# A graph network's two layers on one core: where v's sums lie, when h is moved and turned, and when its sums are made

## Chip, core and metric

The kernel runs on one core of a Trainium2 chip. The metric is the device time of one launch in microseconds (us), the median of three runs. TensorE (PE) multiplies matrices into eight PSUM banks; VectorE (DVE) and ScalarE (ACT) read the banks, add, copy and normalise; GpSimd (POOL) adds a bias; DMA queues move data, most of them issued by SyncE (SP).

## What is computed

x has 64 graphs of 256 nodes with 512 features in fp32, adj is 256 x 256. Both layers end in a residual sum.

```python
h = jnp.maximum(_layernorm(x, axis=-1), 0.0)
q = jnp.einsum('bnd,ed->bne', h, Wq); k = jnp.einsum('bnd,ed->bne', h, Wk)
v = jnp.einsum('bnd,ed->bne', h, Wv)
rel = adj.T[None, :, :] * jnp.einsum('bnd,bmd->bnm', q, k)
rel = rel / jnp.linalg.norm(rel, axis=2, keepdims=True)
x = x + jnp.einsum('bnm,bmd->bnd', rel, v)
h = jnp.maximum(_layernorm(x, axis=-1), 0.0)
x = x + jnp.einsum('bnd,do->bno', jnp.einsum('nm,bmd->bnd', adj, h), weight) + bias
```

## The kernel before

**Pairs and stages.** Two graphs make a pair, so there are 32 pairs. The product Wq' Wk is made once (`m_sb`), so that a pair needs g = h M and scores h g'. `first_pairs` fills a software pipeline, `steady` runs 28 times (i = 1 to 28), and `last_pairs` empties it. One call of `steady` works on four pairs at once, and TensorE goes through five stages in it:

1. `attend_and_v(i, ...)`: rel times v of pair i, between the rest of v of pair i+1 and the last product of the layer-1 mix of pair i-1. With stage 5 this is the double stage.
2. `scores(i+1, ...)`: h g' of pair i+1.
3. `g_and_v(i+2, ...)`, called G here: g of pair i+2 and two products of its v.
4. `gather_steps(i, ...)`: adj times the normalised x of pair i, four products `py` copied to `yt` by ACT (L734).
5. `mix_and_v(i, ...)`: y times the layer-1 weight of pair i, between products of v and g of pair i+2.

**Products by sums.** Every large product is one of seven sub-products ("one" to "seven", written `a1`, `c5`, `a6`, `c3`, `a7`, `b2`, `a4` after their banks), in the order of `winograd_steps` (L183). Products 1, 6, 7 and 4 follow each other in `bank_a`, and each partial sum is read out between two of them: product four may start only when the sum after seven has been read. The operands are sums of blocks that DVE makes beforehand: `left_factors` (L172 to L175, factors 7, 5, 6, 3) and `right_operands` (L134 to L137, factors 7, 5, 6, 4). `two_levels` splits two of the seven once more (`g1` to `g4`, in `bank_e` and `bank_d`); its left sums of h are the four steps of `h_second` (tile `hs`, L172 to L175), those of y are `y_second`.

**Order.** PE, DVE and ACT execute in program order. The dictionaries passed to a stage name what DVE and ACT are given after each of its products ("slots" 0 to 6). So an instruction that waits holds up all that was written behind it on its engine.

**What the change touches.**
- `place_blocks` (L433): sixteen DMAs on SP move h of pair i+3 into `blocks`; `transpose_blocks` (L443) makes eight 32x32-block transposes on DVE (L449) into `ht`, and `sums` are h's four left sums. A load of x stands ahead of `place_blocks` on SP's queue.
- `norm_by_scalar` (L347): the first norm on ACT. Its `root` (L368 on DVE, then a square root on ACT, L369) and `end` (L372, L373) give the scale of h; `relus_of_h` writes h (L376).
- `attend_operands` (L631): the factors of rel and v. The three sums of v are written into `blocks` by way of `spare_blocks`.
- `scores`: `placed` holds the moved rel until `turn` (L587) has turned it in stage 5.
- `ln1`: the second norm, with `halves` (L329, L330), `root`, `end`, `relus` (L341 on ACT), `uppers` (L698 on ACT) and `lowers` (L702 on DVE); `add_bias` (L714) runs on POOL and waits for the relu of the same rows, since it writes them in place.

Of the kernel before, what the change touches and what calls it, by code (L numbers as in the profile page):

```python
# [9 lines left out]
F32 = mybir.dt.float32  # L10
# [9 lines left out]
def kernel(  # L20
# [39 lines left out]
    P = 128  # L60
# [3 lines left out]
    NB = 2  # L64
# [18 lines left out]

    ring = [const.tile([P, NB, NC, D], F32, name=f"x_ring{n}") for n in range(5)]
    blocks = const.tile([P, TC, DC, P], F32, name="blocks")

    def load(i, queue=nc.sync):
        X[i] = ring[i % len(ring)]
# [30 lines left out]
    def flat(t):  # L119
        return t.rearrange("p b c d -> p (b c) d")  # L120
# [420 lines left out]
    def scores(i, side={}, by_matmul=False):  # L541


        left, right = HL.pop(i), G.pop(i)
        rel = work.tile([P, NB, NC, N], F32, tag="rel", name=f"rel_{i}")
        placed = work.tile([P, NB, NC, NC, P], F32, tag="placed", name=f"placed_{i}")
        turned = work.tile([P, NB, NC, NC, P], F32, tag="turned", name=f"turned_{i}")
        rn = small.tile([P, NB, NC], F32, tag="rn", name="rn")
        R[i] = turned, rel

        def take(t, k, bank, first):
            dst = rel[:, :, k, ts(t, P)]
            src = bank[:, :HT_].rearrange("p (b m) -> p b m", b=NB)
            if first:
                nc.scalar.copy(dst, src)  # L555
            else:
                nc.vector.tensor_add(dst, src, dst)  # L557

        def mask(k):
            nc.vector.tensor_mul(  # L560
                rel[:, :, k], rel[:, :, k], adjt_sb[:, k : k + 1, :].to_broadcast([P, NB, N])
            )

        def square_sum(b, k):
            nc.scalar.activation(
                placed[:, b, k].rearrange("p t n -> p (t n)"), rel[:, b, k], AF.Square,
                accum_out=rn[:, b, k : k + 1],
            )

        def root():  # L570
            nc.scalar.activation(rn, rn, AF.Sqrt)

        def inverse():
            nc.vector.reciprocal(rn, rn)

        def scale(b, k):
            nc.scalar.activation(rel[:, b, k], rel[:, b, k], AF.Copy, scale=rn[:, b, k : k + 1])

        def place():
            rv = rel.rearrange("p b k (t m) -> p (b k t) m", m=P)  # L580
            pv = placed.rearrange("p b k t n -> p (b k t) n")
            for j in range(P // S):
                for k in range(P // S):
                    nc.sync.dma_start(out=pv[ts(j, S), :, ts(k, S)], in_=rv[ts(k, S), :, ts(j, S)])

        def turn(b, k):
            nc.vector.transpose(turned[:, b, :, k], placed[:, b, k])  # L587

        def each(f):
            return [(lambda b=b, k=k: f(b, k)) for k in range(NC) for b in range(NB)]  # L590

        def turn_at_once():
            for b in range(NB):
                pt = ps_m.tile([P, T], F32, tag="pm", name="pr")
                for t in range(NC):
                    for k in range(NC):
                        nc.tensor.transpose(
                            pt[:, ts(t * NC + k, P)], rel[:, b, k, ts(t, P)], ident
                        )
                nc.scalar.copy(turned[:, b].rearrange("p t k n -> p (t k n)"), pt)  # L600

        winograd(product_of_tokens(left, right), take, side)
        if by_matmul:
            masks = [lambda: mask(0), lambda: mask(1)]
            return masks, each(square_sum), root, inverse, rn, turn_at_once
        return (
            [lambda: mask(0), lambda: mask(1)], each(square_sum), root, inverse, each(scale), place,
            each(turn),
        )
# [21 lines left out]
    def attend_operands(i):  # L631


        turned, rel = R.pop(i)
        v, t = V.pop(i), spare_blocks()
        room = rel.rearrange("p b k m -> p (b k m)")
        left, left_steps = left_factors(
            lambda n, m: turned[:, :, m, n],
            [room[:, ts(j, HT_)].rearrange("p (b n) -> p b n", b=NB) for j in range(3)],
        )  # L640
        right, right_steps = right_operands(
            lambda m, k: v[:, :, m, ts(k, HD)], t
        )
        R[i] = left, right
        return right_steps, left_steps
# [275 lines left out]
    def first_pairs(exact):  # L921
# [49 lines left out]
        if exact:  # L971
# [11 lines left out]
        run(y_steps[0:2])  # L983
        mixed = mix_and_v(0, g, v, {
            0: y_steps[2:4] + totals[0:2], 1: y_second[0:4] + totals[2:4],
            2: w_second_steps[4:8] + y_second[4:8] + v_steps[0:1] + [mean] + row_squares[0:2],
            3: v_steps[1:4] + row_squares[2:4], 4: sums3[2:3] + turns,
            5: sums3[3:4] + rel_steps[0:2],
        })
        return norm0, rel_steps[2:4], mixed, v  # L990

    def steady(i, exact, norm0, rel_steps, mixed, v):

        gs = g_operands(i + 1)
        root0, end0, relu0 = norm0
        relus0 = relus_of_h(i + 3, relu0)
        stats, root, end, relus, uppers, lowers = ln1(i, exact)  # L1000
        halves = [stats[b * NC + t] for t in range(NC) for b in range(NB)]
        attend_and_v(i, mixed, v, {
            0: rel_steps + [root0, end0], 1: relus0[0:2] + gs[0:1], 2: relus0[2:4] + gs[1:2],
            3: gs[2:3], 4: gs[3:4] + halves[0:1], 5: halves[1:2],
        })
        if i + 4 < NP:
# [2 lines left out]
        HL2.pop(i + 1)  # L1009
        h_second = second_h.pop(i + 2)()  # L1010
        masks, squares, norm_root, inverse, scales, place, turns = scores(i + 1, {
            0: halves[2:3], 1: halves[3:4], 2: [root], 3: [end] + relus[0:1], 4: relus[1:2],
            5: uppers[0:1] + h_second[0:2], 6: uppers[1:2] + h_second[2:4],
        })
        turned, sums = transpose_blocks(i + 3)
        bias_steps = add_bias(i)
        g, v = g_and_v(i + 2, {
            0: masks + squares[0:2] + lowers[0:1],
            1: squares[2:4] + [norm_root] + lowers[1:2],
            2: relus[2:4] + [inverse],  # L1020
            3: scales + [place] + turned[0:2],
            4: uppers[2:4] + lowers[2:3] + turned[2:4] + bias_steps[0:2],
            5: lowers[3:4] + turned[4:8] + bias_steps[2:4], 6: sums[0:2],
        })
        v_steps, rel_steps = attend_operands(i + 1)
        y_products, y_steps = gather_steps(i, exact)
        run_steps(y_products, {
            0: sums[2:3], 1: sums[3:4], 2: y_steps[0:1] + v_steps[0:1], 3: v_steps[1:2],
        })
        y_second = second_of_y(i)  # L1030
        totals, row_squares, mean, norm0 = [], [], [], None
        if i + 4 < NP:
            totals, step, row_squares, *norm0 = norm_by_scalar(flat(X[i + 4]))
            mean = [step]
        run(y_steps[1:2])
        mixed = mix_and_v(i, g, v, {
            0: y_steps[2:4] + totals[0:2], 1: y_second[0:4] + totals[2:4],
            2: y_second[4:8] + mean + row_squares[0:2],
            3: turns + row_squares[2:4], 4: rel_steps[0:2], 5: v_steps[2:4],
        })  # L1040
        return norm0, rel_steps[2:4], mixed, v

    def last_pairs(exact, norm0, rel_steps, mixed, v):

        a, b, c = NP - 3, NP - 2, NP - 1
        gs = g_operands(b)
# [5 lines left out]
        })  # L1052
        h_second = second_h.pop(c)()
        masks, squares, norm_root, inverse, scales, place, turns = scores(b, {
            0: halves[2:3], 1: halves[3:4], 2: [root], 3: [end] + relus[0:1], 4: relus[1:2],
            5: uppers[0:1] + h_second[0:2], 6: uppers[1:2] + h_second[2:4],
        })
        g, v = g_and_v(c, {
            0: masks + squares[0:2] + lowers[0:1],
# [10 lines left out]
            0: gs[0:2] + [v["c"]], 1: gs[2:3], 2: gs[3:4], 3: y_steps[0:1], 4: y_steps[1:3],  # L1070
            5: y_steps[3:4] + turns,
        })
        masks, squares, norm_root, inverse, rn, turn_at_once = scores(
            c, {0: [v["g4"]]}, by_matmul=True
        )
        stats, *parts = ln1(b, exact)
        y_second = second_of_y(a, "hs2")
        attend(b, by_slot({n: [stats[n]] for n in range(TC)}, {
            0: y_second[0:4], 1: masks[0:1], 2: masks[1:2] + squares[0:2],
            3: squares[2:4] + y_second[4:8],  # L1080
        }))
        m = mix_by_two_levels(a)
        root, end, relus, uppers, lowers = parts
# [1 line left out]
            m["a1"], m["c5"], lambda: run([m["a6"], m["c"]]), m["g1"], m["a7"], m["g2"], m["a4"],  # L1085
            m["g3"],
        ], {
            0: [norm_root, root], 1: [inverse, end] + relus[0:2], 2: uppers[0:2],
            3: lowers[0:1] + relus[2:3], 4: lowers[1:2] + relus[3:4],
            5: uppers[2:4] + add_bias(b), 6: lowers[2:3], 7: lowers[3:4],  # L1090
        })
        turn_at_once()
        m["g4"]()
        y_steps = gather(b, exact)
        y_second = second_of_y(b, "hs2")
        stats, *parts = ln1(c, exact)
        attend(c, {
            0: [stats[0], y_steps[0]], 1: [stats[1], y_steps[1]], 2: [stats[2]] + y_steps[2:4],
            3: [stats[3]],
        }, rn)  # L1100
        m = mix_by_two_levels(b)
# [2 lines left out]
            m["a1"], m["c5"], lambda: run([m["a6"], m["c"]]), m["g1"], m["a7"], m["g2"], m["a4"],  # L1104
            m["g3"],
        ], {
            0: y_second[0:4] + [root], 1: y_second[4:8] + [end] + relus[0:2] + uppers[0:2],
            2: lowers[0:1] + relus[2:3], 3: lowers[1:2] + relus[3:4],
            4: uppers[2:4] + add_bias(c), 6: lowers[2:3], 7: lowers[3:4],
        })  # L1110
        y_products, y_steps = gather_steps(c, exact)
# [44 lines left out]
```

## Time and profile before

| | |
|---|---|
| time, median of 3 | 1748.74 us (1748.37 to 1749.79) |
| span of the profiled run | 1746.8 us |
| PE busy | 1694.5 us, 97% |
| DVE busy | 1525.6 us, 87% |
| ACT busy | 807.5 us, 46% |
| POOL busy | 191.9 us, 11% |
| granted TensorE clock | 0.998 |
| one period of `steady` (843.52 to 896.68 us) | 53.16 us: PE 51.99, DVE 47.50, ACT 25.72, POOL 5.96 busy |

"Busy" counts the time in which an instruction of the engine is in flight; matmuls overlap, so PE's share says that it is seldom idle, not that it is at its peak. In the timeline a row gives start, duration, engine, line, operation, and in square brackets how long the engine was idle before it and what ended that. The period repeats to 0.01 us over the run, so that one period stands for 28.

### The profile page before, as it was taken

The page shows a single profiled execution, that of the slowest core. Times are in us where ns is not written, and L with a number is a line of the kernel's source. Part 1 is how long each engine was busy: PE and PEld are TensorE (multiplying, and loading weights), DVE is VectorE, ACT ScalarE, POOL GpSimd, SP SyncE. Part 2 cuts the span into 40 slices and gives each one's busy share as a digit, 9 for nine tenths or more (in the row PEclk, how much of TensorE's full clock was granted, in tenths as well). Part 3 has the DMA queues.
Part 4 walks back from the last instruction along what each step waited for, and adds up shares of the span by engine and source line. Part 5 has one row for each costly group of instructions (what it writes and reads, how often), then busy time and mean ns, then how long its engine had stood idle before and what let it go on. Part 6 is the DMA issues. An engine that isn't in the chain of part 4 may idle for free.

```text
span 1746.8 us, 28457 instructions
## 1 busy us (share of the span) xinstructions
PE 1694.5 (97%) x10274; PEld 1532.8 (88%) x10274; DVE 1525.6 (87%) x3336; ACT 807.5 (46%) x1835; POOL 191.9 (11%) x167
## 2 busy tenths in 40 slices
PE   8999999999999999999999999999999999999997
PEld 7978988889888989888898889898888898888976
DVE  6798899888899888998888998889988889988776
ACT  3445444554445554445544445544455544454331
POOL 0011100111101111001111001110011110011111
PEclk9999999999999999999999999999999999999999
DMA  7413332233322333322333322333223333223101
GB/s 239 63 25 85 75 79 66 37 85 81 78 69 53 61 85 77 79 65 48 72 84 75 74 66 44 85 79 79 69 54 61 85 76 77 67 37 61 33 28 51
DMA packets 425734, 122.56 MB, mean 70 GB/s; under 512 B 398064, under 2 KB 398832, under 8 KB 425584
## 3 DMA queue, kind: packets, MB, share of 16 engines
q1 hardware_dynamic: 412992, 80.28, 24.7%
q0 software_dynamic: 8432, 32.51, 4.9%
q10 hardware_dynamic: 4160, 7.87, 1.3%
q8 instruction: 83, 1.36, 0.3%
q14 instruction: 67, 0.55, 0.1%
HBM read 38.27 MB, written 33.55 MB: 41 GB/s over the span
## 4 chain that ended last, share of the span: by engine, by line
PE 75%; DVE 23%; issue 1%; DMA 0%; ACT 0%; ACTq 0%; DVEq 0%
PE bank_a L298 19%; PE bank_a L286 13%; PE bank_c L298 7%; PE bank_a L310 6%; PE bank_a L653 5%; PE bank_e L524 4%; PE bank_c L286 3%; PE bank_d L524 3%; PE bank_c L310 3%; PE bank_e L477 3%; DVE g L486 3%; DVE x_ring L533 2%; PE bank_b L310 2%; PE bank_d L477 2%; PE bank_c L653 1%; PE bank_b L653 1%
## 5 line engine op out<-in xcount | busy, mean ns | idle before, releaser
L714 POOL TENSOR_TENSOR x_ring<-x_ring,bias_bc 128x512 f32<-128x512 f32 x128 | 167.0, 1325 | 750.1 <-ACT h2c L341 750.1
L298 PE MATMUL bank_a<-wv_t,ht 128*128 128x256 f32 x768 | 181.7, 379 | 0.0
L286 PE MATMUL bank_a<-ht,m_t 128*128 128x256 f32 x768 | 181.4, 379 | 0.0
L286 PEld LDWEIGHTS bank_a<-ht,m_t 128*128 128x128 f32 x768 | 145.9, 190 | 19.8
L298 PEld LDWEIGHTS bank_a<-wv_t,ht 128*128 128x128 f32 x768 | 143.5, 190 | 18.3
L363 ACT ACTIVATE blocks<-x_ring,sm 128x512 f32<-128x512 f32 x112 | 80.8, 722 | 147.2 <-DVE sm L360 145.4
L730 PE MATMUL py<-adjt_r,h 128*128 128x256 f32 x1024 | 126.4, 281 | 0.1
L298 PE MATMUL bank_a<-w_t,ys 128*128 128x256 f32 x512 | 121.5, 380 | 3.4 <-DVE x_ring L764 3.4
L730 PEld LDWEIGHTS py<-adjt_r,h 128*128 128x128 f32 x1024 | 120.5, 188 | 0.3 <-DVE h L702 0.3
L341 ACT ACTIVATE h2c<-x_ring,nb,rs 128x512 f32<-128x512 f32 x128 | 97.4, 807 | 43.9 <-DVE nb L338 39.5
L512 ACT COPY v<-bank_a 128x512 f32<-128x512 f32 x96 | 55.5, 578 | 126.8 <-PE bank_a L298 126.8
L298 PEld LDWEIGHTS bank_a<-w_t,ys 128*128 128x128 f32 x512 | 96.8, 190 | 17.6 <-DVE x_ring L764 4.6
L785 POOL DMA_DIRECT2D out_dram<-x_ring x31 | 24.0, 773 | 783.8 <-issue 568.4
L734 ACT COPY yt<-py 128x512 f32<-128x512 f32 x128 | 75.0, 587 | 72.2 <-PE py L730 54.2
L486 DVE TENSOR_TENSOR g<-bank_e,g 128x256 f32<-128x256 f32 x120 | 50.7, 422 | 61.5 <-ACT g L463 31.1
L310 PE MATMUL bank_a<-ht,gt 128*128 128x128 f32 x744 | 98.4, 275 | 0.4 <-DVE rel L557 0.4
L329 DVE BATCH_NORM_STATS2 st<-x_ring 128x6 f32<-128x512 f32 x144 | 97.9, 680 | 0.4
L555 ACT COPY rel<-bank_a 128x256 f32<-128x256 f32 x96 | 35.4, 369 | 132.3 <-PE bank_a L310 132.3
L764 DVE TENSOR_TENSOR x_ring<-bank_a,x_ring 128x512 f32<-128x512 f32 x128 | 86.9, 679 | 6.6 <-PE bank_a L298 6.5
L310 PEld LDWEIGHTS bank_a<-ht,gt 128*128 128x128 f32 x744 | 90.5, 192 | 0.6 <-DVE rel L557 0.6
L449 DVE STREAM_TRANSPOSE ht<-blocks 128x256 f32<-128x256 f32 x248 | 90.5, 414 | 0.6 <-DMA blocks<-h 0.6
L376 ACT ACTIVATE h<-x_ring,nb,rs 128x512 f32<-128x512 f32 x112 | 82.0, 803 | 14.1 <-PE bank_a L653 12.0
(219 smaller groups left out, 4086.2 us busy)
## 6 DMA issues: line engine op xcount, KB each, us to landing
blocks<-h SPq DMA_DIRECT2D x496, 64.0 KB, 2.3
out_dram<-x_ring POOLq DMA_DIRECT2D x31, 1024.0 KB, 4.7
x_ring<-in_x_dram SPq DMA_DIRECT2D x28, 1024.0 KB, 5.2
placed<-rel SPq DMA_DIRECT2D x496, 32.0 KB, 2.0
x_ring<-in_x_dram ACTq DMA_DIRECT2D x4, 1024.0 KB, 5.3
wq_sb<-in_L_gnn_Wq_dram SPq DMA_DIRECT2D x4, 256.0 KB, 4.8
wk_sb<-in_L_gnn_Wk_dram ACTq DMA_DIRECT2D x4, 256.0 KB, 6.1
wv_sb<-in_L_gnn_Wv_dram ACTq DMA_DIRECT2D x1, 1024.0 KB, 5.2
```

Source lines behind the costliest of these rows:

```text
L286: nc.tensor.matmul(bank[:, e * HT_ : (e + 1) * HT_], right[n][:, d, ts(e, P)], left[n][:, d, :], start=(start and e == 0 and d == 0), stop ...
L298: nc.tensor.matmul(bank[:, b * HD : (b + 1) * HD], left[n][:, d, ts(b, P)], right[n][:, d, :], start=(start and b == 0 and d == 0), stop=( ...
L310: nc.tensor.matmul(bank[:, ts(b, P)], right[n][:, d, ts(b, P)], left[n][:, d, ts(b, P)], start=(start and b == 0 and d == 0), stop=(d == H ...
L329: nc.vector.bn_stats(st[:, c, :], src[:, c, :])
L341: nc.scalar.activation(dst, src[:, c, :], AF.Relu, bias=nb[:, c : c + 1], scale=rs[:, c : c + 1])
L449: nc.vector.transpose(ht[:, d, half].rearrange("p (b n) -> p b n", b=NB), by_half[:, :, half, d])
L477: nc.tensor.matmul(out, m_second[k][n], HL2[i][k][n], start=start, stop=True, skip_group_check=True)
L486: nc.vector.tensor_add(dst, sums, dst)
L524: nc.tensor.matmul(out, left[k][n], right[k][n], start=start, stop=True, skip_group_check=True)
L653: nc.tensor.matmul(bank[:, ts(b, HD)], left[n][:, b], right[n][:, b], start=(start and b == 0), stop=True, skip_group_check=True,)
L714: (lambda c=c: add(xt[:, c, :], xt[:, c, :], bias_bc, ALU.add)) for c in range(TC)
L730: nc.tensor.matmul(pm[:, d, :], left[:, b * NC + m, ts(d0 + d, P)], right, start=(n == 0), stop=(n == len(terms) - 1),)
```

## The change

It gives the sums of v a room of their own, so that `blocks` is free for h earlier, and with that it reorders the work of DVE and ACT:

- Two of v's sums lie in `placed` (free once rel is turned), one in a new tile `v_room`. The sums 0 and 1 of v are made in slot 5 of G rather than in the gather stage.
- `root0` and `end0` of the next h are made in slot 4 of stage 5 rather than in slot 0 of stage 1, and its relus one slot earlier.
- h is turned as a whole in slot 1 of G (eight transposes, ahead of `inverse`) rather than in slots 3 to 5; its four sums come in slots 3 and 4 of G rather than in slot 6 and the gather stage.
- In `scores` the steps of `h_second` move from slots 5 and 6 to slots 1 and 2.
- In `last_pairs` the steps of `y_second` and `norm_root`, and the y sums of pair b, move to other slots. `first_pairs` is reordered likewise.

```diff
+    v_room = const.tile([P, D], F32, name="v_room")
...
-        R[i] = turned, rel
+        R[i] = turned, rel, placed
...
-        turned, rel = R.pop(i)
-        v, t = V.pop(i), spare_blocks()
+        turned, rel, placed = R.pop(i)
+        v, spare = V.pop(i), placed.rearrange("p b k t n -> p (b k t n)")
+        t = [
+            r.rearrange("p (b n) -> p b n", b=NB) for r in (spare[:, :D], v_room, spare[:, D:])
+        ]
...
         attend_and_v(i, mixed, v, {
-            0: rel_steps + [root0, end0], 1: relus0[0:2] + gs[0:1], 2: relus0[2:4] + gs[1:2],
+            0: rel_steps + relus0[0:2], 1: relus0[2:4] + gs[0:1], 2: gs[1:2],
             3: gs[2:3], 4: gs[3:4] + halves[0:1], 5: halves[1:2],
...
         masks, squares, norm_root, inverse, scales, place, turns = scores(i + 1, {
-            0: halves[2:3], 1: halves[3:4], 2: [root], 3: [end] + relus[0:1], 4: relus[1:2],
-            5: uppers[0:1] + h_second[0:2], 6: uppers[1:2] + h_second[2:4],
+            0: halves[2:3], 1: halves[3:4] + h_second[0:1], 2: [root] + h_second[1:4],
+            3: [end] + relus[0:1], 4: relus[1:2], 5: uppers[0:1], 6: uppers[1:2],
         })
...
+        v_steps, rel_steps = attend_operands(i + 1)
         g, v = g_and_v(i + 2, {
             0: masks + squares[0:2] + lowers[0:1],
-            1: squares[2:4] + [norm_root] + lowers[1:2],
-            2: relus[2:4] + [inverse],
-            3: scales + [place] + turned[0:2],
-            4: uppers[2:4] + lowers[2:3] + turned[2:4] + bias_steps[0:2],
-            5: lowers[3:4] + turned[4:8] + bias_steps[2:4], 6: sums[0:2],
-        })
-        v_steps, rel_steps = attend_operands(i + 1)
+            1: squares[2:4] + [norm_root] + lowers[1:2] + turned + [inverse],
+            2: relus[2:4],
+            3: scales + [place] + sums[0:2],
+            4: uppers[2:4] + lowers[2:3] + sums[2:4] + bias_steps,
+            5: lowers[3:4] + v_steps[0:2],
+        })
         y_products, y_steps = gather_steps(i, exact)
-        run_steps(y_products, {
-            0: sums[2:3], 1: sums[3:4], 2: y_steps[0:1] + v_steps[0:1], 3: v_steps[1:2],
-        })
+        run_steps(y_products, {2: y_steps[0:1]})
...
-            totals, step, row_squares, *norm0 = norm_by_scalar(flat(X[i + 4]))
-            mean = [step]
+            totals, step, row_squares, root0, end0, relu0 = norm_by_scalar(flat(X[i + 4]))
+            mean, ends = [step], [root0, end0]
...
-            3: turns + row_squares[2:4], 4: rel_steps[0:2], 5: v_steps[2:4],
+            3: turns + row_squares[2:4], 4: rel_steps[0:2] + ends, 5: v_steps[2:4],
...
         masks, squares, norm_root, inverse, rn, turn_at_once = scores(
-            c, {0: [v["g4"]]}, by_matmul=True
+            c, {0: [v["g4"]], 1: y_second[0:4], 2: y_second[4:8]}, by_matmul=True
         )
...
         attend(b, by_slot({n: [stats[n]] for n in range(TC)}, {
-            0: y_second[0:4], 1: masks[0:1], 2: masks[1:2] + squares[0:2],
-            3: squares[2:4] + y_second[4:8],
+            0: masks[0:1], 1: masks[1:2] + squares[0:2], 2: squares[2:4], 3: [norm_root],
         }))
...
-            0: y_second[0:4] + [root], 1: y_second[4:8] + [end] + relus[0:2] + uppers[0:2],
-            2: lowers[0:1] + relus[2:3], 3: lowers[1:2] + relus[3:4],
+            0: y_second[0:4] + [root], 1: [end] + relus[0:2] + uppers[0:2],
+            2: y_second[4:8] + lowers[0:1] + relus[2:3], 3: lowers[1:2] + relus[3:4],
```

More of the change, by code (lines that the diff above doesn't have):

```diff
@@ L985, in first_pairs, with steady @@
             0: y_steps[2:4] + totals[0:2], 1: y_second[0:4] + totals[2:4],
-            2: w_second_steps[4:8] + y_second[4:8] + v_steps[0:1] + [mean] + row_squares[0:2],
-            3: v_steps[1:4] + row_squares[2:4], 4: sums3[2:3] + turns,
-            5: sums3[3:4] + rel_steps[0:2],
-        })
-        return norm0, rel_steps[2:4], mixed, v
-    def steady(i, exact, norm0, rel_steps, mixed, v):
+            2: w_second_steps[4:8] + y_second[4:8] + [mean] + row_squares[0:2],
+            3: v_steps[0:2] + row_squares[2:4], 4: turns + rel_steps[0:2] + norm0[0:2],
+            5: v_steps[2:4] + sums3[2:4],
+        })
+        return norm0[2], rel_steps[2:4], mixed, v
+    def steady(i, exact, relu0, rel_steps, mixed, v):
         gs = g_operands(i + 1)
-        root0, end0, relu0 = norm0
         relus0 = relus_of_h(i + 3, relu0)
@@ L1016, in steady @@
         bias_steps = add_bias(i)
+        v_steps, rel_steps = attend_operands(i + 1)
         g, v = g_and_v(i + 2, {
             0: masks + squares[0:2] + lowers[0:1],
-            1: squares[2:4] + [norm_root] + lowers[1:2],
-            2: relus[2:4] + [inverse],
-            3: scales + [place] + turned[0:2],
-            4: uppers[2:4] + lowers[2:3] + turned[2:4] + bias_steps[0:2],
-            5: lowers[3:4] + turned[4:8] + bias_steps[2:4], 6: sums[0:2],
+            1: squares[2:4] + [norm_root] + lowers[1:2] + turned + [inverse],
[3 more added lines that the diff above has]
+            5: lowers[3:4] + v_steps[0:2],
         })
-        v_steps, rel_steps = attend_operands(i + 1)
         y_products, y_steps = gather_steps(i, exact)
-        run_steps(y_products, {
-            0: sums[2:3], 1: sums[3:4], 2: y_steps[0:1] + v_steps[0:1], 3: v_steps[1:2],
-        })
+        run_steps(y_products, {2: y_steps[0:1]})
         y_second = second_of_y(i)
-        totals, row_squares, mean, norm0 = [], [], [], None
+        totals, row_squares, mean, ends, relu0 = [], [], [], [], None
         if i + 4 < NP:
-            totals, step, row_squares, *norm0 = norm_by_scalar(flat(X[i + 4]))
-            mean = [step]
+            totals, step, row_squares, root0, end0, relu0 = norm_by_scalar(flat(X[i + 4]))
+            mean, ends = [step], [root0, end0]
         run(y_steps[1:2])
@@ L1038, in steady, with last_pairs @@
             2: y_second[4:8] + mean + row_squares[0:2],
-            3: turns + row_squares[2:4], 4: rel_steps[0:2], 5: v_steps[2:4],
+            3: turns + row_squares[2:4], 4: rel_steps[0:2] + ends, 5: v_steps[2:4],
         })
-        return norm0, rel_steps[2:4], mixed, v
-    def last_pairs(exact, norm0, rel_steps, mixed, v):
+        return relu0, rel_steps[2:4], mixed, v
+    def last_pairs(exact, relu0, rel_steps, mixed, v):
         a, b, c = NP - 3, NP - 2, NP - 1
@@ L1054, in last_pairs @@
         masks, squares, norm_root, inverse, scales, place, turns = scores(b, {
-            0: halves[2:3], 1: halves[3:4], 2: [root], 3: [end] + relus[0:1], 4: relus[1:2],
-            5: uppers[0:1] + h_second[0:2], 6: uppers[1:2] + h_second[2:4],
+            0: halves[2:3], 1: halves[3:4] + h_second[0:1], 2: [root] + h_second[1:4],
+            3: [end] + relus[0:1], 4: relus[1:2], 5: uppers[0:1], 6: uppers[1:2],
         })
@@ L1072, in last_pairs @@
         })
+        y_second = second_of_y(a, "hs2")
         masks, squares, norm_root, inverse, rn, turn_at_once = scores(
-            c, {0: [v["g4"]]}, by_matmul=True
+            c, {0: [v["g4"]], 1: y_second[0:4], 2: y_second[4:8]}, by_matmul=True
         )
         stats, *parts = ln1(b, exact)
-        y_second = second_of_y(a, "hs2")
         attend(b, by_slot({n: [stats[n]] for n in range(TC)}, {
-            0: y_second[0:4], 1: masks[0:1], 2: masks[1:2] + squares[0:2],
-            3: squares[2:4] + y_second[4:8],
+            0: masks[0:1], 1: masks[1:2] + squares[0:2], 2: squares[2:4], 3: [norm_root],
         }))
@@ L1087, in last_pairs @@
         ], {
-            0: [norm_root, root], 1: [inverse, end] + relus[0:2], 2: uppers[0:2],
+            0: [root], 1: [inverse, end] + relus[0:2], 2: uppers[0:2],
             3: lowers[0:1] + relus[2:3], 4: lowers[1:2] + relus[3:4],
@@ L1093, in last_pairs @@
         m["g4"]()
-        y_steps = gather(b, exact)
+        y_products, y_steps = gather_steps(b, exact)
+        run_steps(y_products, {2: y_steps[0:1]})
         y_second = second_of_y(b, "hs2")
@@ L1097, in last_pairs @@
         attend(c, {
-            0: [stats[0], y_steps[0]], 1: [stats[1], y_steps[1]], 2: [stats[2]] + y_steps[2:4],
+            0: [stats[0], y_steps[1]], 1: [stats[1], y_steps[2]], 2: [stats[2], y_steps[3]],
             3: [stats[3]],
```

## The prediction

> **What bounds the kernel now.** I read the busy shares first: PE 97%, DVE 87%. Then the chain of waits, which names what is left between PE's instructions.
>
> ```profile
> PE 1694.5 (97%) x10274; PEld 1532.8 (88%) x10274; DVE 1525.6 (87%) x3336; ACT 807.5 (46%) x1835; POOL 191.9 (11%) x167
> ...
> PE 75%; DVE 23%; issue 1%; DMA 0%; ACT 0%; ACTq 0%; DVEq 0%
> ```
>
> PE carries three quarters of the chain and DVE nearly all of the rest: at some places of each period PE waits for DVE. PE's timeline of one period (53.16 us, from 843.52) finds them.
>
> ```profile
> 861.77 1.89 PE L298 MATMUL bank_a<-w_sb,yt 128*128 128x256 f32 x8
> 864.47 1.97 PE L298 MATMUL bank_c<-w_sb,yt 128*128 128x256 f32 x8 [0.81 <-DVE yt L173]
> ...
> 878.92 0.61 PE L524 MATMUL bank_d<-wvt_sb,hs 128*128 128x128 f32 x4
> 879.88 1.13 PE L653 MATMUL bank_a<-blocks,rel 128*128 128x256 f32 x4 [0.34 <-DVE rel L174]
> ...
> 888.23 0.61 PE L524 MATMUL bank_d<-wvt_sb,ht 128*128 128x128 f32 x4
> 888.85 1.13 PE L653 MATMUL bank_a<-blocks,turned 128*128 128x256 f32 x4
> ```
>
> Unhindered, eight 256-column matmuls start 1.73 us apart, four of 128 columns 0.445. So mix product c5 could start at 863.50 and is 0.97 late, attend's six at 879.37 and is 0.51 late, attend's four at 888.67 and is 0.18 late; each refills more slowly too, by 0.07 to 0.10. Together 1.93 us per period, and that is all PE loses: over 28 periods 54 us is the most that any reordering of DVE can win here.
>
> DVE's timeline shows why c5 waits, and what its own slow places are.
>
> ```profile
> 843.00 1.14 DVE L172 TENSOR_TENSOR hs<-ht 128x256 f32<-128x256 f32 x1
> 844.07 1.48 DVE L173 TENSOR_TENSOR hs<-ht 128x256 f32<-128x256 f32 x1
> ...
> 861.10 0.69 DVE L175 TENSOR_TENSOR ht<-ht 128x512 f32<-128x512 f32 x1
> 861.71 0.68 DVE L172 TENSOR_TENSOR ys<-yt 128x512 f32<-128x512 f32 x1
> 862.31 0.68 DVE L134 TENSOR_TENSOR blocks<-v 128x512 f32<-128x512 f32 x1
> 863.03 0.69 DVE L135 TENSOR_TENSOR v<-v 128x512 f32<-128x512 f32 x1
> 863.64 0.68 DVE L173 TENSOR_TENSOR yt<-yt 128x512 f32<-128x512 f32 x1
> ...
> 880.20 0.16 DVE L368 TENSOR_SCALAR sq<-sq 128x4 f32<-128x4 f32 x1
> 880.63 0.18 DVE L372 RECIPROCAL rs<-rs 128x4 f32<-128x4 f32 x1 [0.27 <-ACT rs L369]
> 880.85 0.16 DVE L373 TENSOR_TENSOR nb<-sm,rs 128x4 f32<-128x4 f32 x1
> ```
>
> The yt sum that c5 needs stands behind h's four sums and two of v. And `h_second`'s first two steps take 1.14 and 1.48 us, where the same forms take 0.42 in the first call (98.43, 98.76). POOL's timeline gives the reason:
>
> ```profile
> 842.60 2.67 POOL L714 TENSOR_TENSOR x_ring<-x_ring,bias_bc 128x512 f32<-128x512 f32 x2 [14.95 <-ACT h2c L341]
> ```
>
> Both lie inside POOL's two bias adds. Each ends 0.21 to 0.28 us after one of them.
>
> **What the Trainium skill says.** "SBUF — State Buffer", Who interferes with whom: a DVE instruction with two SBUF inputs contends with a GpSimd instruction that reads SBUF, and the later one blocks. The trace agrees: 0.42 becomes 1.14 and 1.48 beside POOL, while transposes (one input) and reads of PSUM keep their times at 850.79 to 853.3, beside the second pair of bias adds. "PSUM — Partial Sum Buffer", Engine vs sequencer instructions: DVE and ACT are strict first-in first-out; DVE's order in the trace is that of the slots. Same page, PSUM bank collisions: a bank has to be guarded as a whole, so product four waits for the read after seven; the trace has it at 888.85, just after L660 ends at 888.80, and at 87.16 in `scores`, where four waited 0.41 for L557.
>
> **The change, part by part** (us on the clock of the period above; a DVE step followed by an independent one costs 0.60 for 512 columns, 0.33 for 256, a dependent one 0.72 and 0.45).
>
> 1. *Gather and mix.* Four h sums (2.8) and two v sums (1.3) leave the gather stage. The last copy of `yt` ends at 862.55, L173 then starts at 862.58; before, 0.83 lay between L173's start and c5's, so c5 is fed by 863.41, ahead of 863.50. Gain 0.97 + 0.07 = 1.04.
>
> 2. *`root0` and `end0` in mix slot 4.* From L368 to the next instruction they take 0.72 (880.20 to 880.92), of which 0.27 is DVE waiting for ACT's root. Between 873.88, where DVE waits for PE (`g4`), and 879.82, where L174 feeds six, DVE never idles. So the trio pushes everything behind it (four reads of x, two v sums, L174), and six starts 0.72 later against PE's other work: cost 0.72. Behind L174 the trio is gone, so DVE is where it was (L660 at 880.93 against 880.92). Seven, now 0.72 later, ends at 888.67, L660 reads it by 889.40 and four could start at 889.40: the wait at four is gone, and four moves from 888.85 to 889.43. Net cost in attend 0.58. The alternative to this, that it is hidden, needs idle DVE in that stretch, and there is none.
>
> 3. *`h_second` in slots 1 and 2 of `scores`.* POOL's adds start only after relu L341 (895.75), so at 893 the port is free, and I take 0.42 each: L172 892.97, L333 893.30, L173 893.38, L174 893.83, L175 894.29. Queued behind them are L557 for c3 (894.63, before 894.11), `end` (894.97 to 895.25) and L557 for a7, ending at 895.67. Product four wants 895.62: it waits about 0.1, plus 0.1 of refill. Cost 0.2. If all were as slow as before (1.07 + 1.52 to the next start instead of 0.33 + 0.45), L557 would end at 897.5 and the wait would be 2.0.
>
> 4. *G.* With a1 of G at 0: relus come 0.5 later, POOL's first adds fall on -0.4 to 2.2, so the first mask (two SBUF inputs) ends near 2.7, the second at 3.3, two lowers by 4.5, eight transposes (0.333 each) by 7.15, `inverse`, two g1 adds by 7.95 (before 7.35), two h sums by 10.4 (one blocked by POOL's second adds), c and a7 by 11.5, while a4 needs a7's read at 12.15. Then g2, lower, two sums, lower (14.4; the second gather product needs it at 15.6), two v sums (15.75), g3's adds by 16.8 (before 15.6). PE waits nowhere, unless a gather product takes the bank that the last add frees: 0 to 0.4. I take 0.1. L173 of the gather stage can start at 19.2, so 2 us of DVE room remain, enough for L172 (0.68).
>
> 5. *h's move.* Its relus end about 881, but the sixteen DMAs stand behind the load of x on SP (884.86). Issue takes 11.4 (890.05 to 901.42), landing 2.3: they are done by 898.9, and the transposes want them near 901. The x load (5.2) shares the engines; still hidden. New rooms for v's sums cost nothing: `placed` is free after `turns`, `v_room` is last read by seven. ACT (25.72 of 53.16 busy) hides the earlier relus.
>
> Sum per period: -1.04 + 0.58 + 0.2 + 0.1 = -0.16, over 28 periods -4.5. The last `steady` call has no next norm, so 0.7 more is won there.
>
> 6. *`last_pairs`.* `y_second` (2 x 1.03) in `scores(c)` delays L557 of a7 to 1673.86, against four at 1673.42: cost 0.5. Without it in `attend(b)` the read of mix a1 comes near 1684.9 instead of 1686.3, so a6 no longer waits 1.58 (+0.17): start 1685.1 against 1686.38, net gain 1.25 after that cost. In pair c's attend one y sum less ahead of a1's read (0.6 of the 1.05 wait), and a6's read ahead of `y_second[4:8]` (1.05) removes most of the 0.78 wait before a7; the two overlap with later waits for ACT: gain about 1. Together -2.2. `first_pairs`: L173 and L174 of rel change places with h and v sums in one queue: 0.
>
> Total -4.5 - 0.7 - 2.2 = -7.4: 1748.7 - 7.4 = 1741.
>
> **Rivals.**
> - *More is won.* The trio hides after all and nothing waits in `scores`: -1.04 and the 0.28 of four per period, 28 x -1.3 = -36 and -3 at the end, at best 1710; with half of it, about 1724. For it: DVE totals 47.50 of 53.16, so there is room on average. Against: no idle DVE from 873.88 to 879.82.
> - *DVE backlog in G (slower).* G's queue gets 4.1 us more and had only 2.65 idle; if the locks or a late h add 1 to 2 us, c5's wait returns or the gather products wait for a bank: +0.88 per period, 25 - 3 gives about 1771; a mild form, about 1757. For it: part 4 ends 1.2 later than before. Against: 2 us remain ahead of L173.
> - *`h_second` stays slow (slower).* If not POOL but reading `ht` beside PE makes it slow: +1.8 per period, 50 - 7, about 1791. Against: 0.42 at 98.43 with PE reading `ht` as well, and 0.41 at 1640.30 just as POOL starts.
> - *Cancels.* The delays of parts 2 to 4 add up to 1.04: 1746.
>
> **How the numbers follow.** Forecast with its small variations (1734 to 1745) 45%, more won 20%, cancels 13%, backlog 17%, `h_second` slow 5%. The predicted time is 1741. The range 1720 to 1762 takes in half of the larger gain and a mild backlog. Faster by over 0.2% (below 1745.2): forecast nearly whole and more won, 0.62; within: 0.16; slower (above 1752.2): 0.22.
>
> **What would show it.** Right: c5 of mix without a wait for L173, six waiting about 1.2 for L174, four of attend with none, a four in `scores` that waits 0.1 to 0.3 for L557, `hs` steps of 0.42, a period near 53.0. Wrong: any wait of PE in G or gather, `hs` steps over 1 us in `scores`, the transposes L449 waiting for the DMA of h, or six no later than before.

## The result, and the profile after

| | before | after |
|---|---|---|
| time, median of 4 runs each on the same chip | 1748.55 us (1748.24 to 1749.79) | 1742.72 us (1741.9 to 1743.3) |
| span of the profiled run | 1746.8 us | 1740.6 us |
| mean period of `steady` (second to 29th gather) | 53.16 us | 52.92 us |

The ratio is 0.9965 with a 95% interval of 0.9948 to 0.9982: faster by a third of a per cent. Lines of the kernel after are one higher than before's from L86 on and five higher from L636 on; the edits of the experiments shift the later lines by a few, at most nine.

These are the busy shares and the chain of waits of the kernel after:

```profile
PE 1698.9 (98%) x10274; PEld 1531.7 (88%) x10274; DVE 1523.9 (88%) x3336; ACT 818.3 (47%) x1835; POOL 198.2 (11%) x167
...
PE 84%; DVE 14%; issue 1%; ACT 0%; DMA 0%; ACTq 0%; DVEq 0%
```

PE's part of the chain has risen from 75% to 84% and DVE's has fallen from 23% to 14%, so some waits for DVE are gone, and not all. PE's timeline of one period says which. G begins in it at 840.65 and again at 893.67 us: it is one of six longer periods (53.02 instead of 52.89), in which the gather products take 3.86 us instead of 3.73.

```profile
859.20 1.89 PE L299 MATMUL bank_a<-w_sb,yt 128*128 128x256 f32 x8
860.92 1.90 PE L299 MATMUL bank_c<-w_sb,yt 128*128 128x256 f32 x8
...
873.79 0.49 PE L525 MATMUL bank_e<-w_t,yt 128*128 128x128 f32 x2
...
875.64 0.61 PE L525 MATMUL bank_d<-wvt_sb,hs 128*128 128x128 f32 x4
...
876.98 1.13 PE L658 MATMUL bank_a<-placed,rel 128*128 128x256 f32 x4 [0.72 <-DVE rel L175]
...
885.33 0.61 PE L525 MATMUL bank_d<-wvt_sb,ht 128*128 128x128 f32 x4
885.83 1.13 PE L658 MATMUL bank_a<-placed,turned 128*128 128x256 f32 x4
...
891.71 1.06 PE L311 MATMUL bank_b<-ht,g 128*128 128x128 f32 x8
892.68 1.16 PE L311 MATMUL bank_a<-ht,gt 128*128 128x128 f32 x8
```

Mix product c5 follows its predecessor after 1.72 us and waits no longer. Attend's six, 0.445 after its predecessor if unhindered, is now 0.89 late (876.98 - 876.09; before 0.51), and `g4` ahead of it loses another 0.24 and refills 0.1 longer. Four of attend is 0.05 late instead of 0.18, and four of `scores` (892.68) is 0.08 late and takes 1.16 instead of 1.06.

DVE's timeline shows the two things that the change was to mend, and a new one:

```profile
841.63 2.23 DVE L561 TENSOR_TENSOR rel<-rel,adjt_sb 128x512 f32<-128x512 f32 x2 [1.42 <-ACT rel L556]
...
849.27 1.65 DVE L174 TENSOR_TENSOR ht<-ht 128x512 f32<-128x512 f32 x1
...
858.13 0.69 DVE L173 TENSOR_TENSOR ys<-yt 128x512 f32<-128x512 f32 x1 [0.89 <-ACT yt L739]
860.01 0.69 DVE L174 TENSOR_TENSOR yt<-yt 128x512 f32<-128x512 f32 x1 [1.19 <-ACT yt L739]
...
872.42 0.18 DVE L373 RECIPROCAL rs<-rs 128x4 f32<-128x4 f32 x1 [0.27 <-ACT rs L370]
...
876.50 0.42 DVE L175 TENSOR_TENSOR rel<-turned 128x256 f32<-128x256 f32 x1
...
889.95 0.39 DVE L173 TENSOR_TENSOR hs<-ht 128x256 f32<-128x256 f32 x1
890.33 0.42 DVE L174 TENSOR_TENSOR hs<-ht 128x256 f32<-128x256 f32 x1
```

The yt sum now finds DVE idle (0.89 and 1.19 us), and `h_second`'s first steps take 0.4 instead of 1.14 and 1.48. In their place the masks of rel (a mean of 1106 ns instead of 683) and two sums of h (means of 879 and 1528 ns instead of 680 and 692) lie beside POOL's bias adds. The root and end, with their 0.27 of idling (872.42), now lie ahead of L175, which feeds six.

The ledger by the first gather product of each pair: it starts 0.63 us earlier for the first pair; the next interval is 1.36 longer (58.58 against 57.22); the 27 periods after that win 6.58; the last three intervals change by -0.91, -0.77 and +1.44, and the tail by -0.1. The sum is -6.2. The first 0.63 is no gain of the change: the kernel of the fifth experiment, which is before's up to that point, starts its first gather at 109.08 us, just as the kernel after does, where before started it at 109.71; over all eleven traces this start scatters from 109.03 to 110.79.

### The profile page after: what moved, and what is told of

The parts are those of the page before. It is cut to its first block, busy times and chain, and to the rows that moved or that the text cites. A ratio compares the mean times of both kernels' runs of the same rounds, so it can differ in the third digit from the quotient of the medians.

```text
span 1740.6 us, 28453 instructions
## 1 busy us (share of the span) xinstructions
PE 1698.9 (98%) x10274; PEld 1531.7 (88%) x10274; DVE 1523.9 (88%) x3336; ACT 818.3 (47%) x1835; POOL 198.2 (11%) x167
## 3 DMA queue, kind: packets, MB, share of 16 engines
q8 instruction: 83, 1.36, 0.3%
## 4 chain that ended last, share of the span: by engine, by line
PE 84%; DVE 14%; issue 1%; ACT 0%; DMA 0%; ACTq 0%; DVEq 0%
PE bank_a L299 22%; PE bank_a L287 13%; PE bank_a L311 7%; PE py L735 6%; PE bank_c L299 6%; PE bank_a L658 5%; PE bank_e L525 4%; PE bank_c L287 3%; PE bank_e L478 3%; PE bank_d L525 3%; PE bank_c L311 3%; PE bank_d L478 2%; DVE x_ring L534 2%; PE bank_b L311 2%; DVE x_ring L769 1%; PE bank_b L658 1%
## 5 line engine op out<-in xcount | busy, mean ns | idle before, releaser
L719 POOL TENSOR_TENSOR x_ring<-x_ring,bias_bc 128x512 f32<-128x512 f32 x128 | 173.2, 1374 | 736.5 <-DVE rel L558 443.8
L769 DVE TENSOR_TENSOR x_ring<-bank_a,x_ring 128x512 f32<-128x512 f32 x128 | 86.9, 679 | 21.7 <-PE bank_a L299 21.5
L561 DVE TENSOR_TENSOR rel<-rel,adjt_sb 128x512 f32<-128x512 f32 x64 | 68.4, 1106 | 41.3 <-ACT rel L556 41.3
L665 DVE TENSOR_TENSOR x_ring<-bank_a,x_ring 128x512 f32<-128x512 f32 x116 | 78.8, 679 | 10.7 <-PE bank_a L658 10.7
```

The lines of the kernel that those rows point to most:

```text
L719: (lambda c=c: add(xt[:, c, :], xt[:, c, :], bias_bc, ALU.add)) for c in range(TC)
L769: nc.vector.tensor_add(xt[block], bank.rearrange("p (b e) -> p b e", b=NB), xt[block])
```

## Experiments

The runs of before beside them had medians of 1748.70, 1748.64 and 1748.56 us, one for each group of runs.

### The trio alone goes back

```diff
-            3: turns + row_squares[2:4], 4: rel_steps[0:2] + ends, 5: v_steps[2:4],
+            3: turns + row_squares[2:4], 4: rel_steps[0:2], 5: v_steps[2:4],
...
-            0: rel_steps + relus0[0:2], 1: relus0[2:4] + gs[0:1], 2: gs[1:2],
+            0: rel_steps + ends0 + relus0[0:2], 1: relus0[2:4] + gs[0:1], 2: gs[1:2],
```

The trio (the three DVE instructions of `root0` and `end0`: L369, L373, L374) goes back in `first_pairs` in the same way; the lines that hand the steps over are left out here.

> The changed kernel with root0 and end0 back in slot 0 of attend, behind the four sums of rel. Theory (DVE never idles between g4 and L175, so the trio delays six): L175 comes 0.72 earlier, six starts about 0.7 earlier (876.25 in place of 876.98 on the period's clock), four about 0.5 earlier; period 52.4 in place of 52.9, time 1728 to 1731. Rival (the trio has to come early so that h is moved in time): its relus start about 1 us later, the transposes L450 in G wait for the DMA of h, and the time is 1742 or more.

Measured: 1726.57 us (1725.47 to 1728.08), ratio 0.9876 (0.9859 to 0.9892), mean period 52.32, 0.6 below the kernel after. Six waits a visible 0.34 instead of 0.72:

```profile
867.76 1.13 PE L658 MATMUL bank_a<-placed,rel 128*128 128x256 f32 x4 [0.34 <-DVE rel L175]
```

And `g4` follows its predecessor after 0.87 us, without a delay. So `root0` and `end0` in slot 4 cost 0.6 per period, and without that edit the change is worth 1.2%. The first interval, which has the same trio in `first_pairs`, falls from 58.58 to 57.96.

### `h_second` goes back to slots 5 and 6

```diff
-            0: halves[2:3], 1: halves[3:4] + h_second[0:1], 2: [root] + h_second[1:4],
-            3: [end] + relus[0:1], 4: relus[1:2], 5: uppers[0:1], 6: uppers[1:2],
+            0: halves[2:3], 1: halves[3:4], 2: [root], 3: [end] + relus[0:1], 4: relus[1:2],
+            5: uppers[0:1] + h_second[0:2], 6: uppers[1:2] + h_second[2:4],
```

The same lines change in `last_pairs`.

> The changed kernel with h_second back in slots 5 and 6 of scores. Theory: four of scores no longer waits (0.2 per period won); two hs steps lie beside POOL's bias adds again and take over 1 us, the masks come free of them, G's queue ends about 1 us later, which the 2.1 us of DVE idle ahead of the yt sum L174 take up: period 0.2 shorter, about 1737 to 1739. Rival (G is full, h_second had to leave it): c5 of mix or a product of G waits, 1745 to 1760.

Measured: 1751.26 us (1748.52 to 1754.94), ratio 1.0013 (1.0004 to 1.0022), mean period 53.18. The theory was wrong and the rival right. DVE's and then PE's timeline of this run, in G:

```profile
846.24 1.14 DVE L173 TENSOR_TENSOR hs<-ht 128x256 f32<-128x256 f32 x1
847.30 1.49 DVE L174 TENSOR_TENSOR hs<-ht 128x256 f32<-128x256 f32 x1
...
855.37 1.71 DVE L173 TENSOR_TENSOR ht<-ht 128x512 f32<-128x512 f32 x1
...
858.33 0.68 DVE L466 TENSOR_TENSOR g<-bank_a,g 128x512 f32<-128x512 f32 x1
```

```profile
857.01 1.89 PE L299 MATMUL bank_c<-wvt_sb,ht 128*128 128x256 f32 x8
859.06 1.99 PE L287 MATMUL bank_a<-ht,m_t 128*128 128x256 f32 x8 [0.16 <-DVE g L466]
```

The steps of `hs` are slow again, the queue behind them is late, and product four of G, due at 857.01 + 1.73 = 858.74, starts at 859.06, when the read of `bank_a` after seven (858.33 to 859.01) is over. That is 0.32 late, with 0.1 of refill; 0.18 is won back at four of `scores`; the net 0.24 is the difference of the periods (53.13 against 52.89 in the usual period). The first interval is longer too, 60.56 against 58.58; what makes it so was not traced. I had judged G's room by the 2 us that DVE idles at its end. The room that counts lies in its middle: in the kernel after, the same read ends at 852.12 and four starts at 852.80, 0.68 later.

### The sums of v in `blocks` again

```diff
-        v, spare = V.pop(i), placed.rearrange("p b k t n -> p (b k t n)")
-        t = [
-            r.rearrange("p (b n) -> p b n", b=NB) for r in (spare[:, :D], v_room, spare[:, D:])
-        ]
+        v, t = V.pop(i), spare_blocks()
```

> The changed kernel with v's sums in blocks again. Theory (the room is what lets h be moved early): the DMAs of h start only after four of attend (886.8), land at about 900.5 where the transposes want 898.0; DVE waits about 2.5 us in slot 1 of G, and PE about 1.9 per period behind it: 1790, at least 1765. Rival (h's move was hidden anyway): within 5 us of the changed kernel.

Measured: 1757.73 us (1757.26 to 1760.15), ratio 1.0055 (1.0038 to 1.0072). The periods scatter from 52.88 to 54.41 with a mean of 53.47, which is 0.55 above the kernel after: the direction is right, the size is a third of what I expected. This is SyncE's queue and then a part of DVE's timeline of this run:

```profile
890.89 0.38 SPq L90 DMA_DIRECT2D x_ring<-in_x_dram  x1
895.78 11.33 SPq L440 DMA_DIRECT2D blocks<-h  x16
```

```profile
855.45 2.73 DVE L450 STREAM_TRANSPOSE ht<-blocks 128x256 f32<-128x256 f32 x8 [1.79 <-DMA blocks<-h]
```

The move of h (here that of the next period) now starts 4.9 us after the load of x, when product four of attend, which reads `blocks`, is over (894.58 to 895.71), and DVE idles 1.79 us for it ahead of the transposes. Little of that reaches PE in this period: the two sums of h behind the transposes now miss the bias adds (0.67 and 0.69 instead of 0.91 and 1.65), and the read after seven ends 0.67 us later in G than in the kernel after, which had 0.68 to spare. Product four of G is 0.05 late (861.46) and refills 0.1 longer. In the longest period, 54.41 us, DVE waits longer, and PE too:

```profile
480.70 2.73 DVE L450 STREAM_TRANSPOSE ht<-blocks 128x256 f32<-128x256 f32 x8 [3.16 <-DMA blocks<-h]
...
483.41 0.39 DVE L487 TENSOR_TENSOR g<-bank_e,g 128x256 f32<-128x256 f32 x1
```

```profile
480.92 1.89 PE L287 MATMUL bank_a<-ht,m_t 128*128 128x256 f32 x8
483.85 0.71 PE L478 MATMUL bank_e<-hs,m_t 128*128 128x128 f32 x4 [1.04 <-DVE g L487]
```

The product in `bank_e`, due at 482.65, is 1.20 late with 0.1 of refill, and four is 0.13 late with 0.1: 1.53 together, and 54.41 - 52.89 = 1.52. So the room for the sums of v is what lets h be turned early: without it the early turning stalls DVE, and PE pays for what exceeds the room in G.

### Before, without the bias adds

```diff
-        return [
-            (lambda c=c: add(xt[:, c, :], xt[:, c, :], bias_bc, ALU.add)) for c in range(TC)
-        ]
+        return [lambda: None for c in range(TC)]
```

> The kernel before without the bias adds on POOL (the bias is left out of the result). Theory (port lock): the hs steps L172 and L173 take 0.42 in place of 1.14 and 1.48, and since DVE waits for PE at the end of G in any case, the period stays at 53.16 and the time within 2 us of 1748. Rival (they are slow because PE reads ht at that time): they stay over 1 us.

DVE's timeline of this run, `h_second` in its old place:

```profile
844.17 0.42 DVE L172 TENSOR_TENSOR hs<-ht 128x256 f32<-128x256 f32 x1
844.51 0.42 DVE L173 TENSOR_TENSOR hs<-ht 128x256 f32<-128x256 f32 x1
```

Without POOL's adds the steps take 0.42 where they took 1.14 and 1.48. That the adds slow them is thereby shown; that the two engines contend for SBUF when a DVE instruction has two inputs there is what "SBUF — State Buffer", Who interferes with whom, of the Trainium skill states. The time did not fall with it: 1753.19 us (1752.95 to 1756.92), ratio 1.0029 (1.0018 to 1.0041), period 53.30 against 53.16. So in before those slow steps cost PE nothing. The 0.14 more goes with L368, which takes 0.31 us (a mean of 315 ns over its 28 calls) instead of 0.16 and stands ahead of the read that four of attend waits for (0.33 late instead of 0.18):

```profile
881.37 0.31 DVE L368 TENSOR_SCALAR sq<-sq 128x4 f32<-128x4 f32 x1
```

Why L368 takes longer stays open.

### Before, with `h_second` early and nothing else

```diff
-            0: halves[2:3], 1: halves[3:4], 2: [root], 3: [end] + relus[0:1], 4: relus[1:2],
-            5: uppers[0:1] + h_second[0:2], 6: uppers[1:2] + h_second[2:4],
+            0: halves[2:3], 1: halves[3:4] + h_second[0:1], 2: [root] + h_second[1:4],
+            3: [end] + relus[0:1], 4: relus[1:2], 5: uppers[0:1], 6: uppers[1:2],
```

The same lines change in `last_pairs`.

> The kernel before with h_second alone moved to slots 1 and 2 of scores. Theory: hs steps 0.42 each, four of scores waits about 0.1 for L557 and refills 0.1 slower, the room won in G is idle DVE: period 53.36, time about 1754. Rival (DVE's total is the bound): the 1.8 us of lock time taken out show as a shorter period, under 1740.

Measured: 1754.28 us (1753.5 to 1756.46), ratio 1.0033 (1.0019 to 1.0047), mean period 53.34: 0.18 more than before, as expected: four of `scores` is 0.08 late with 0.1 of refill. The same edit costs 0.18 per period in the kernel before and saves 0.24 in the kernel after (the second experiment). Before, the slow steps put 1.8 us more in front of a G that had room for them. After, six more of the transposes and two sums of h stand ahead of the read that product four of G waits for, and it has not.

### The ends in another order

In `first_pairs` the sums of h and v go ahead of the rel sums in the last slots of the mix; in `last_pairs` the second half of `y_second` of pair b goes back by one slot.

```diff
-            2: w_second_steps[4:8] + y_second[4:8] + [mean] + row_squares[0:2],
-            3: v_steps[0:2] + row_squares[2:4], 4: turns + rel_steps[0:2] + norm0[0:2],
-            5: v_steps[2:4] + sums3[2:4],
+            2: w_second_steps[4:8] + y_second[4:8] + v_steps[0:1] + [mean] + row_squares[0:2],
+            3: v_steps[1:2] + row_squares[2:4], 4: sums3[2:3] + turns + v_steps[2:4],
+            5: sums3[3:4] + rel_steps[0:2] + norm0[0:2],
...
-            0: y_second[0:4] + [root], 1: [end] + relus[0:2] + uppers[0:2],
-            2: y_second[4:8] + lowers[0:1] + relus[2:3], 3: lowers[1:2] + relus[3:4],
+            0: y_second[0:4] + [root], 1: y_second[4:8] + [end] + relus[0:2] + uppers[0:2],
+            2: lowers[0:1] + relus[2:3], 3: lowers[1:2] + relus[3:4],
```

> The changed kernel with first_pairs' mix slots in the old order (new rooms kept) and y_second[4:8] of pair b back in slot 1 of mix b. Theory: 1.3 us at the start (six and g4 of the first double stage) and 1.4 us at the end (the wait of 2.41 ahead of g2) come back: about 1740. Rival (the new order pays elsewhere in these stages): 1742 to 1744.

Measured: 1742.1 us (1740.3 to 1743.82), ratio 0.9961 (0.9947 to 0.9975). The last interval falls from 27.56 to 25.37, and the first rises from 58.58 to 59.78: one half right, one wrong. What had gone wrong at the end is seen in the kernel after, on DVE, POOL and PE:

```profile
1706.73 1.02 DVE L175 TENSOR_TENSOR ys<-yt 128x128 f32<-128x128 f32 x1
1707.79 1.24 DVE L176 TENSOR_TENSOR ys<-yt,ys 128x128 f32<-128x128 f32 x1
```

```profile
1706.34 2.54 POOL L719 TENSOR_TENSOR x_ring<-x_ring,bias_bc 128x512 f32<-128x512 f32 x2 [15.17 <-ACT h2c L342]
```

```profile
1710.55 0.71 PE L525 MATMUL bank_e<-w_t,ys 128*128 128x128 f32 x4 [2.41 <-DVE x_ring L534]
```

Two steps of `y_second`, which take 0.28 us elsewhere, take 1.02 and 1.24 inside POOL's bias adds, and PE then waits 2.41 us for the read of x queued behind them. With the steps back by one slot they take 0.28 and 0.29, ahead of POOL's adds, and PE waits 0.61, as in before:

```profile
1706.72 0.29 DVE L176 TENSOR_TENSOR ys<-yt,ys 128x128 f32<-128x128 f32 x1
```

```profile
1711.08 0.71 PE L525 MATMUL bank_e<-w_t,ys 128*128 128x128 f32 x4 [0.61 <-DVE x_ring L534]
```

The change took `h_second` out from beside the bias adds and put `y_second` there.

### The sums of v ahead of attend

The third sum of v is made at the end of the gather stage, in a room behind `ys2`, and the fourth after the rel sums in attend; neither lies ahead of L175 any more. The lines that hand the room over are left out here.

```diff
-        run(y_steps[1:2])
+        run(y_steps[1:2] + v_steps[2:3])
...
-            3: turns + row_squares[2:4], 4: rel_steps[0:2] + ends, 5: v_steps[2:4],
+            3: turns + row_squares[2:4], 4: rel_steps[0:2] + ends,
...
-        return relu0, rel_steps[2:4], mixed, v
+        return relu0, rel_steps[2:4] + v_steps[3:4], mixed, v
```

> The changed kernel with v's sum 2 (factor 6) made at the end of the gather stage, into room behind ys2 in the h2 tile, and sum 3 (factor 4) behind the sums of rel in attend. Theory (six waits for DVE's queue alone, and DVE has idle time before mix): L175 comes 1.3 earlier, six starts without a wait, four about 1.0 earlier: period 51.9, time about 1715. Rival (DVE is full from mix to attend, so that work moved from ahead of six only shifts the wait to seven, four or a6): period above 52.5, time above 1732.

Measured: 1718.37 us (1716.18 to 1719.07), ratio 0.9826 (0.9809 to 0.9842), usual period 51.92 as expected. Six now follows its predecessor after 0.44 us. The trio stays in slot 4, and its cost has become smaller, not nothing; PE's timeline of a period has it at `g4`:

```profile
860.44 1.03 PE L662 MATMUL bank_a<-v,turned 128*128 128x256 f32 x4
861.55 0.49 PE L525 MATMUL bank_e<-w_t,yt 128*128 128x128 f32 x2
```

In the run with the trio back 0.87 lay between these two starts, here 1.11, and `g4` refills 0.1 longer: 0.34 per period, as in the kernel after. The read of `bank_e` that stands behind the trio ends at 861.49.

### All together, and then with `first_pairs` left alone

The sums of v as above; `root0` in slot 4 and `end0` behind the rel sums; the ends as in the run of the ends.

> The kernel of the run before with, besides, root0 alone in slot 4 of mix and end0 behind the sums of rel in attend (so that DVE does not wait for ACT's root), and both ends as in the run that restores them. Theory: the 0.34 that g4 of mix loses is won too, 9 us, and 2.7 at the ends: about 1703. Rival (full DVE): above 1725.

Measured: 1708.56 us (1705.02 to 1711.78), ratio 0.9762 (0.9745 to 0.9778), usual period 51.58 or 51.70. Against the run before, 51.92 - 51.58 = 0.34 is won: `end0`, with its wait for ACT's root, no longer stands ahead of the read that `g4` needs. The first interval is 61.1 us. The last run therefore leaves the slots of `first_pairs` as the change has them, but for its root and end:

```diff
-            3: v_steps[0:2] + row_squares[2:4], 4: turns + rel_steps[0:2] + norm0[0:2],
+            3: v_steps[0:2] + row_squares[2:4], 4: turns + rel_steps[0:2],
...
-        return norm0[2], rel_steps[2:4], mixed, v
+        return (norm0[2], norm0[0:2]), rel_steps[2:4], mixed, v
...
-            0: rel_steps + relus0[0:2], 1: relus0[2:4] + gs[0:1], 2: gs[1:2],
+            0: rel_steps[0:2] + ends0 + rel_steps[2:] + relus0[0:2], 1: relus0[2:4] + gs[0:1], 2: gs[1:2],
```

> Same as the run with everything together, but first_pairs keeps the slots of the changed kernel, and its root and end follow the first pair of rel sums of attend in slot 0. Theory: the first interval, from the first gather to the second, which took 61.1 us there, comes near the 57.96 us of the run with the trio alone moved back; the steady periods stay at 51.58 to 51.70 and the last interval at 25.4; time 1708.6 - 3 = 1705 to 1706. Rival: the first interval is long because v's third and fourth sums, now also made late, and the first pair's sums of h fill one queue whatever the order; then it stays above 60 and the time at 1708 to 1709.

Measured: 1706.6 us (1705.08 to 1706.8), ratio 0.9756 (0.9743 to 0.9769). The first interval is 59.53, between the two theories: what remains over 57.96 is not settled. The time alone does not tell the last two runs apart, as their ranges overlap. The busy shares, the chain of waits, and one period by engine (length; busy PE, PEld, DVE, ACT, POOL; clock; DMA) of this last kernel:

```profile
PE 1685.9 (99%) x10274; PEld 1532.4 (90%) x10274; DVE 1513.4 (89%) x3336; ACT 818.2 (48%) x1835; POOL 198.1 (12%) x167
...
PE 94%; DVE 4%; issue 0%; DMA 0%; ACT 0%; ACTq 0%; DVEq 0%
```

```profile
843.50:895.08 51.58, 51.58 (x322) 47.39 (x321) 47.09 (x105) 26.05 (x59) 6.22 (x5) 1.00 0.34 73
```

PE is busy for all of the 51.58 us. The prediction's unhindered period is 53.16 - 1.93 = 51.23, so 0.35 of the 1.93 remains. The view shows no idle time in it, but the starts do, at four of attend and four of `scores`:

```profile
869.04 0.61 PE L525 MATMUL bank_d<-wvt_sb,ht 128*128 128x128 f32 x4
869.54 1.13 PE L662 MATMUL bank_a<-placed,turned 128*128 128x256 f32 x4
...
875.42 1.06 PE L311 MATMUL bank_b<-ht,g 128*128 128x128 f32 x8
876.38 1.16 PE L311 MATMUL bank_a<-ht,gt 128*128 128x128 f32 x8
```

They are 0.05 and 0.07 late, and each refills 0.1 longer: 0.32 together.

## Why the prediction came out as it did

The total was right (1741 forecast, 1742.7 measured), and in the period so were the mechanisms. In the two ends the forecast missed, and an error of the other sign in the period's sum (step 4, 0.1 in each period) and the 0.6 at the start made up for most of it. That the total came within 2 us is in this part luck.

1. *Gather and mix* (1.04): c5 waits no longer, and the yt sum finds DVE idle. Right.
2. *The trio* (net 0.58): six and `g4` together are now 0.89 + 0.34 = 1.23 late against 0.51, a step of the 0.72 forecast. Taking the trio back won 0.6. Right in the sum, and shown by the run; the forecast put all 0.72 at six, and the trace has 0.34 of it at `g4`. That VectorE's queue is strictly first in, first out is what "PSUM — Partial Sum Buffer", Engine vs sequencer instructions, of the Trainium skill says, so that an instruction that waits for ACT holds up all behind it; the 0.27 at 872.42 is such a wait.
3. *`h_second`* (0.2): 0.42 a step, four of `scores` 0.08 late with 0.1 of refill. Right in time and, by the run without bias adds, in cause.
4. *G* (0.1): PE waits nowhere in it, so 0. With that the sum is -0.26, and 52.89 is measured in the usual period against 53.16. The step had both numbers, 0.65 us before a4 and 2 us at the end; that the smaller one is the room was shown only by the run with `h_second` late, where it was used up.
5. *h's move* (0): hidden, though in another order than forecast: the relus of h end at 877.24, not near 881. SP's queue shows four of the sixteen DMAs issued ahead of the load of x:

```profile
877.27 4.92 SPq L440 DMA_DIRECT2D blocks<-h  x4
882.65 0.37 SPq L90 DMA_DIRECT2D x_ring<-in_x_dram  x1
883.06 10.63 SPq L440 DMA_DIRECT2D blocks<-h  x12
```

6. *The ends* (-2.2, and 0 in `first_pairs`) is the step that failed. The last `steady` call won its 0.7 (53.08 to 52.17, with the period's gain). Then pair b and pair c together came out at -0.77 + 1.44 - 0.1 = +0.57 instead of -2.2: I had counted the `y_second` steps by their number and not asked what POOL does beside them, though step 3 rests on just that. Put back by one slot, they give back 2.2. `first_pairs` came out at +1.36 instead of 0 (the 0.63 before it is not the change's). Of the 1.36, 0.62 is its own trio in slot 4 (the first run). The other order of its sums that I tried was worse by 1.2, so what the rest is stays open.

In the forecast's sum: 27 periods gave 6.6 instead of 4.3, the last `steady` call 0.9 as forecast (its period's gain and 0.7), and the two ends cost 1.36 + 0.57 = 1.9 instead of winning 2.2. With the 0.6 at the start that is 6.2 in the span instead of 7.4.

Of the rivals, "more is won" did not come, because the trio does not hide, as its counter-argument said; the last run, with the sums of v and the root and end elsewhere, shows that a gain of that size was there to be had, 1706.6 against the 1710 of that rival at best. "DVE backlog in G" did not come either, but the run with `h_second` late is its mild form. "`h_second` stays slow" is refuted by the steps of 0.4.

## What to carry over

- The room of an engine off the path is the smallest distance from one of its results to the instruction that needs it, not the idle time at the end of a stage. Check each bank read that a product waits for.
- A short chain over two engines (0.72 us on DVE, 0.27 of it idle) is placed behind the last result that the bound engine wants, not ahead of it; the same edit cost 0.6 us per period here, still 0.34 once two other steps had left the stretch, and nothing that the starts of six and `g4` show once only its first step stood there.
- Before moving an addition with two SBUF inputs, look at what POOL does at its new time: 0.28 us became 1.24.

## What was not expected of the hardware

- The gather products of a period take 3.73 us or 3.86 us, and either may come in any period (6 of 28 are long in the kernel after). In before the wait of c5 absorbed the difference, and each period was 53.16; in the kernel after they are 52.89 and 53.02. The cause is not known.
- L368, 128x4 elements, has a mean of 0.16 us in before, after and eight other runs, and of 0.31 us in the one without bias adds.
- The sixteen moves of h, which the load of x now divides, take 3.6 us (median) from issue to landing instead of 2.3.
